# Gather indices through a small ScalarE copy, and one product moved ahead of the dot product's sum

## The chip, the cores and the metric

The kernel runs on one NeuronCore of a Trainium2 chip. The metric is the device time of one execution in microseconds (us). Before the change it is 5222.7 us, the median of three runs (5202.25 to 5230.44). The profile that is read here comes from one execution of its own: 5204.84 us in all, 5203.0 us from the first to the last instruction of the program.

## What is computed

One layer of an equivariant graph network: 12,500 nodes of 160 features (64 scalars, 32 vectors of three parts) and 400,000 edges, sorted by their target. Each edge takes the mapped row `y` of its source node, weighs it with weights that a small network makes from 16 edge features, multiplies it with four further edge features, and adds it to its target node.

```python
h = jnp.maximum(_layernorm(x, axis=-1), 0.0)
y0, y1 = x0 @ W_l1_0, einsum('nuc,uv->nvc', x1, W_l1_1)      # per node
w = silu(edge_length_embedded @ fc_W1) @ fc_W2                # per edge: w_a, w_b, w_c, w_d
ys0, ys1 = y0[edge_src], y1[edge_src]                         # the gather
mid_a = w_a * ys0 * e0
mid_d = w_d * einsum('euc,ec->eu', ys1, e1)                   # the dot product
mid_b = (w_b * ys0)[:, :, None] * e1[:, None, :]
mid_c = (w_c * e0)[:, :, None] * ys1
z = zeros.at[edge_dst].add(concatenate(mid_a, mid_d, mid_b, mid_c))
out = x + C_S * s + C_X * (z @ W_l2)
```

## The kernel before

**Stages.** A first stage (to about 218 us) normalises the nodes and writes `y` to the table `y_d` in HBM. The edge stage takes all the rest. A short last stage stores what is left.

**Tiles and batches.** 128 edges make a tile, four tiles a batch (`GT` = 4): 3125 tiles, 782 batches. In 22 of them (every 32nd) the rows are made again on the core instead of being gathered (`made`); the other 760 batches are gathered, by 3037 gathers of 128 rows of 640 bytes (the last batch is shorter).

**Edge stage.** One Python loop over `b` (L774) writes out the order of three engines by hand:

- **TensorE (PE)**: `weigh(b + 2)` makes the weights of a batch in the PSUM bank `pw` (L566, eight matmul passes; there are two such banks). `sums(b)` adds the finished products of a batch into `pz` through selection matrices (L603). `turn`, `map_sums` (every four batches or so) and `hidden` (every second batch, L550) use two further banks `px`.
- **ScalarE (ACT)**: `weigh` ends with a copy of three edge features next to the weights in `pw` (L567). This copy waits for the matmuls of its batch, and the queue is in order, so everything behind it waits too: what leaves PSUM (`all_leave`: `zs` L609, `za` L621, `os` L634 and L635, `hT` L555), then the four lifts of the batch (`lift_rows`, `yge`, L484).
- **VectorE (DVE)**: `dots_of(b + 1)` multiplies (L489) and sums (L491) the dot product; `products(b + 1)` makes `both` (L495), and then four pieces of `pr` (L496, L497, L500, L501). `weigh` may write a `pw` bank again when L501 of the batch that used it is done.
- **GpSimd (POOL)**: `load(b + 8)` issues the four gathers of a batch (L540). Its queue is not in the hand-written order, but it runs in program order. Each gather reads its row numbers from a column of `src_sb`.
- **SyncE (SP)** loads the edge features (`xe`, `raw`).

**What a gather waits for.** The gathered rows lie in nine buffers (`yg`, L135). Batch `c` takes the buffer that the ninth gathered batch before it had. Its first gather waits until VectorE has read that one for the last time (`both`, L495) and ScalarE has lifted it (L484). So within the loop the gathers that are issued in the code for batch `b + 10` follow, in time, `both` and the lift of batch `b + 1`. The other three gathers of a batch wait for nothing that is late.

Of the kernel before, what the change touches and what calls it, by code (L numbers as in the profile page):

```python
# [10 lines left out]
F32 = mybir.dt.float32  # L11
I32 = mybir.dt.int32
AF = mybir.ActivationFunctionType
# [5 lines left out]
P = 128  # L19
M0 = 64  # L20
M1 = 32
# [5 lines left out]
GT = 4  # L27
BT = 32
WN = 128
TG = 12  # L30
EG = 8
WIDE = 3, 5
GN = 8
HN = 2
# [9 lines left out]
def kernel(  # L44
# [19 lines left out]
    nc = tc.nc  # L64
# [11 lines left out]
    NB = (T + GT - 1) // GT  # L76
# [28 lines left out]
    def made(b):  # L105

        return b // RS - 1 if b % RS == 0 and 0 < b <= nr * RS else None
# [20 lines left out]
    src_sb = const.tile([P, TP], I32, name="src_sb")  # L128
# [3 lines left out]
    tile_i = const.tile([P, NG], I32, name="tile_i")  # L132
    far_i = const.tile([1, 1], I32, name="far_i")

    ygp = ctx.enter_context(tc.tile_pool(name="yg", bufs=9))  # L135

    ld = ctx.enter_context(tc.tile_pool(name="ld", bufs=2))
    NQ = -(-NU // EG)
# [126 lines left out]
    def load_xe(blk):  # L265

        if blk not in blocks:
            xe = ld.tile([P, 512], F32, name="xe")
            v = e16[blk * P:(blk + 1) * P, :].rearrange("(s k f) (h c) -> k s (f h) c", s=4, k=2, h=2)
            for k in range(2):  # L270
                nc.sync.dma_start(xe[:, 256 * k:256 * (k + 1)], v[k])
            blocks[blk] = xe
# [210 lines left out]
        for k in range(n):  # L483
            nc.scalar.activation(yge[:, k, :], yg[:, k, :], AF.Copy, scale=e4v[:, k, 0:1])  # L484

    def dot(tmp, wt, yg, n):

        y1 = yg[:, :n, M0:].rearrange("p t (c u) -> p t c u", c=3)
        nc.vector.tensor_tensor(tmp[:, :n, 0:3, :], y1, wt[:, :n, NW:NW + 3].unsqueeze(3).to_broadcast([P, n, 3, M1]),  # L489
                                ALU.mult)  # L490
        nc.vector.tensor_reduce(tmp[:, :n, 3, :], tmp[:, :n, 0:3, :].rearrange("p t c u -> p t u c"), AX.X, ALU.add)  # L491

    def multiply(pr, both, tmp, wt, yg, yge, n):

        nc.vector.tensor_mul(both[:, :n, :], wt[:, :n, 96:160], yg[:, :n, 0:M0])  # L495
# [5 lines left out]
        nc.vector.tensor_mul(pr[:, :n, 96:192].rearrange("p t (c u) -> p t c u", c=3),  # L501
                             wt[:, :n, M0:96].unsqueeze(2).to_broadcast([P, n, 3, M1]),
                             yge[:, :n, M0:].rearrange("p t (c u) -> p t c u", c=3))

    with (
# [3 lines left out]
        tc.tile_pool(name="hid", bufs=4) as hid,  # L509
        tc.tile_pool(name="post", bufs=2) as post,  # L510
        tc.tile_pool(name="made", bufs=2) as mk,
        tc.tile_pool(name="banks", bufs=1, space=PSUM) as banks,
    ):
        (hids, rows, lifted, dots, wts, sels, z_ps, z_sb, zT, o_sb, prs) = ({} for _ in range(11))
        leaving = []
        pws = [banks.tile([P, GT, 256], F32, name=f"pw{i}") for i in range(2)]
        pzs = [banks.tile([P, 512], F32, name=f"pz{i}") for i in range(2)]
        pxs = [banks.tile([P, 512], F32, name=f"px{i}") for i in range(2)]
# [4 lines left out]
            return pxs[turns["px"] % 2]  # L523

        K = TG // GT
        AHEAD = 8

        def tiles_of(b):
            return list(range(b * GT, min((b + 1) * GT, T)))

        def load(b):
            load_xe(b * GT // BT)
            r = made(b)
            if r is not None:
                rows[b] = xms[r]
                return
            yg = ygp.tile([P, GT, D], F32, name="yg")
            rows[b] = yg
            for k, t in enumerate(tiles_of(b)):
                nc.gpsimd.indirect_dma_start(  # L540
                    out=yg[:, k, :], out_offset=None, in_=y_d,
                    in_offset=bass.IndirectOffsetOnAxis(ap=src_sb[:, t:t + 1], axis=0))

        def hidden(s):

# [12 lines left out]
        def weigh(b):  # L558
            hT = hids[b // 2]
            pw = pws[b % 2]  # L560
            n = len(tiles_of(b))
            for k in (0, 2, 1, 3):
                if k < n:
                    r = slice(FC_H * (k // 2), FC_H * (k // 2 + 1))
                    o = P * (b % 2 * 2 + k % 2)
                    nc.tensor.matmul(pw[:, k, 0:NW], hT[r, o:o + P], w2[r, :], start=True, stop=True)  # L566
            nc.scalar.activation(pw[:, :n, NW:NW + 3], e4_of(b)[:, :n, 1:4], AF.Copy)  # L567
            wts[b] = pw
# [10 lines left out]
        def select(u, pz):  # L579

            n = min(TG, T - u * TG)
            sels[u] = selp.tile([P, TG, WN], F32, name="sel")
            nc.vector.tensor_tensor(sels[u][:, 0:n, :], pz[:, ZC:].unsqueeze(1).to_broadcast([P, n, WN]),  # L583
                                    drel[:, u * TG:u * TG + n].unsqueeze(2).to_broadcast([P, n, WN]), ALU.is_equal)

        def dots_of(b):
            dots[b] = part.tile([P, GT, 4, M1], F32, name="tmp")
            dot(dots[b], wts[b], rows[b], len(tiles_of(b)))

        def products(b):  # L590
            pr = prod.tile([P, GT, ZC], F32, name="pr")
            both = part.tile([P, GT, M0], F32, name="both")
            multiply(pr, both, dots.pop(b), wts.pop(b), rows.pop(b), lifted.pop(b), len(tiles_of(b)))
            prs[b] = pr

        def sums(b):
# [146 lines left out]
        def all_leave():  # L743
            todo = leaving[:]
            leaving.clear()
            for f in todo:
                f()

        order = tc.manual_schedule(engines={mybir.EngineType.PE, mybir.EngineType.Activation, mybir.EngineType.DVE})
        with order:  # L750
            e4_load(0)
            for b in range(min(AHEAD, NB)):
                load(b)
            relate_edges(0, part, lim)
            for s in range(3):
                hidden(s)
                all_leave()
            if NQ == 1:
                any_far(next_px()[0:1, 0:1])
            for b in range(min(2, NB)):  # L760
                weigh(b)
                lift_rows(b)
            for pz in pzs:
                nc.vector.tensor_copy(pz[:, ZC:], iota[:, 0:WN])
            dots_of(0)
            products(0)
            select(0, pzs[0])
            last_batch = [(t - 1) // GT for t in ends]
            turns_at, maps_at, adds_at = {}, {}, {}
            for g, e in enumerate(last_batch):  # L770
                turns_at.setdefault(e + 1, []).append(g)
                maps_at.setdefault(e + 2, []).append(g)
                adds_at.setdefault(e + (4 if e + 4 < NB else 3), []).append(g)
            for b in range(NB + 3):  # L774
                u, k = divmod(b, K)
                due(at_start, b)
                if b + AHEAD < NB:
                    load(b + AHEAD)
                if b < NB:
                    q, r = divmod(b, EG * K)  # L780
                    if r == 0:
                        e4_load(q + 1)
                    if r == EG * K - 8 and q + 1 < NQ:
                        relate_edges(q + 1, part, lim)
                    if r == EG * K - 4 and q + 2 == NQ:
                        any_far(next_px()[0:1, 0:1])
                if b + 2 < NB:
                    weigh(b + 2)
                all_leave()
                due(on_scalar, b)  # L790
# [24 lines left out]
    with (  # L815
# [11 lines left out]
        with tc.For_i(0, n, 1) as _:  # L827
# [4 lines left out]
            with tc.For_i(0, TP // GT, 1) as g:  # L832
# [31 lines left out]
                dot(tmp, pw, yg, GT)  # L864
                pr = fp.tile([P, GT, ZC], F32, name="f_pr")
                both = fp.tile([P, GT, M0], F32, name="f_both")
                multiply(pr, both, tmp, pw, yg, yge, GT)
# [81 lines left out]
```

## Time and profile before

| | |
|---|---|
| time, median of three runs | 5222.7 us (5202.25 to 5230.44) |
| the profiled execution: its time, its span | 5204.84 us, 5203.0 us |
| mean granted TensorE clock | 0.857 of full speed |
| gathers, packets moved by their queue | 3037 in the edge stage, 256.20 MB in all |
| DMA traffic | 64 GB/s over the span |

In a timeline row stand: start in us, duration in us, engine, line, operation, tiles (output <- inputs), shapes, how many instructions the row merges, and in brackets the idle time of that engine just before and what ended it. "issue" as the one that ended it means that the profile shows no event that did. In a group row the numbers behind the bar are the busy time, the mean of one instruction in ns, and the idle time before the group's instructions with what ended most of it. In the rows of one source line the three numbers with slashes are the shortest, median and longest duration in ns, and behind them the first and last start in us. In the list of waits a row gives the sum in us, how many waits, and the longest.

### The profile page before, as it was taken

The numbers are of one execution on the slowest core, as the hardware profiler recorded it, in microseconds if no ns is written. First come the engines' busy times: TensorE is split into PE (matmuls) and PEld (weight loads), VectorE is DVE, ScalarE is ACT, GpSimd is POOL, SyncE is SP. The second block draws the span as 40 slices with busy tenths as digits, with TensorE's granted clock in tenths as the row PEclk, the third lists the DMA queues.
The fourth block names the chain that finished last, engine by engine and source line by source line (L and its number), as shares of the span: only waits on it lengthen the run. The fifth ranks groups of instructions, "written<-read, shape, count | busy, mean of one in ns | idle before, by whom it ended". The sixth has DMA issues, their size and how long they took to land. (4 is left out here: it accounts for less than half of the span.)

```text
span 5203.0 us, 55078 instructions
## 1 busy us (share of the span) xinstructions
PE 4180.4 (80%) x16329; PEld 2384.2 (46%) x16329; DVE 3441.9 (66%) x7529; ACT 1764.7 (34%) x5580; POOL 2959.6 (57%) x3137
## 2 busy tenths in 40 slices
PE   4478888787888888888888878888888888888888
PEld 3334444444444444444444444444444444544444
DVE  4456667666666666776666666676767666766667
ACT  3323333333333333332333333333333333333333
POOL 4455655555555555555555555555555555655553
PEclk7778888888888888888888888888888888888888
DMA  5322222222222222222222222222222222232222
GB/s 180 115 57 58 61 58 62 58 60 60 57 60 59 60 61 57 59 61 60 57 60 58 60 57 57 60 60 58 60 54 61 58 59 57 61 94 57 57 57 58
DMA packets 227720, 333.84 MB, mean 64 GB/s; under 512 B 54714, under 2 KB 171526, under 8 KB 227158
## 3 DMA queue, kind: packets, MB, share of 16 engines
q0 software_dynamic: 150000, 256.20, 19.9%
q1 hardware_dynamic: 63618, 65.63, 4.0%
q10 hardware_dynamic: 13796, 8.44, 0.5%
q8 instruction: 130, 2.13, 0.2%
q14 instruction: 176, 1.44, 0.1%
HBM read 306.83 MB, written 23.22 MB: 63 GB/s over the span
## 5 line engine op out<-in xcount | busy, mean ns | idle before, releaser
L540 POOL DMA_INDIRECT yg<-y_d,src_sb x3037 | 2871.3, 945 | 2115.7 <-ACT yge L484 784.9
L603 PE MATMUL pz<-pr,sel 128*128 128x384 f32 x6250 | 2510.0, 548 | 58.4 <-issue 54.7
L603 PEld LDWEIGHTS pz<-pr,sel 128*128 128x128 f32 x6250 | 1259.2, 212 | 1032.0 <-issue 491.5
L489 DVE TENSOR_TENSOR tmp<-yg,pw 128x384 f32<-128x384 f32 x760 | 418.6, 551 | 1523.1 <-ACT pw L567 1292.7
L567 ACT ACTIVATE pw<-raw 128x12 f32<-128x12 f32 x782 | 141.9, 182 | 3289.3 <-issue 2801.2
L484 ACT ACTIVATE yge<-yg,raw 128x160 f32<-128x160 f32 x3037 | 1044.0, 421 | 0.0
L566 PE MATMUL pw<-w,hT 64*128 64x192 f32 x6250 | 839.5, 392 | 73.7 <-issue 24.1
L566 PEld LDWEIGHTS pw<-w,hT 64*128 64x128 f32 x6250 | 572.6, 212 | 545.1 <-issue 313.4
L497 DVE TENSOR_TENSOR pr<-both,pw 128x768 f32<-128x768 f32 x782 | 737.9, 944 | 0.0
L550 PE MATMUL px<-xe,w 32*128 32x512 f32 x782 | 522.9, 756 | 189.4 <-ACT os L635 137.1
L491 DVE TENSOR_REDUCE tmp<-tmp 128x128 f32<-128x384 f32 x782 | 464.1, 594 | 26.9
L583 DVE TENSOR_TENSOR sel<-pz,drel 128x1536 f32<-128x1536 f32 (+1 forms) x261 | 455.2, 1744 | 0.0
L501 DVE TENSOR_TENSOR pr<-pw,yge 128x384 f32<-128x384 f32 x782 | 428.0, 547 | 0.0
L617 PE MATMUL px<-ident,zs 128*128 128x128 f32 x555 | 112.7, 319 | 358.9 <-ACT zs L609 341.3
L500 DVE TENSOR_TENSOR pr<-pw,yge 128x256 f32<-128x256 f32 x782 | 326.6, 418 | 13.0 <-ACT yge L484 12.3
L495 DVE TENSOR_TENSOR both<-pw,yg 128x256 f32<-128x256 f32 x760 | 314.8, 414 | 0.0
L550 PEld LDWEIGHTS px<-xe,w 32*128 32x128 f32 x782 | 130.7, 209 | 345.5 <-ACT os L635 163.4
L630 PE MATMUL px<-wc,za 128*128 128x96 f32 x1110 | 165.5, 289 | 145.3 <-ACT za L621 137.7
L617 PEld LDWEIGHTS px<-ident,zs 128*128 128x128 f32 x555 | 74.2, 159 | 446.9 <-ACT zs L609 395.9
L630 PEld LDWEIGHTS px<-wc,za 128*128 128x128 f32 x1110 | 161.5, 205 | 207.4 <-ACT za L621 155.1
L555 ACT ACTIVATE hT<-px 128x512 f32<-128x512 f32 x391 | 229.3, 587 | 1.9 <-PE px L550 1.7
L496 DVE TENSOR_TENSOR pr<-pw,tmp 128x128 f32<-128x128 f32 x782 | 219.4, 281 | 0.0
(118 smaller groups left out, 1739.2 us busy)
## 6 DMA issues: line engine op xcount, KB each, us to landing
yg<-y_d,src_sb POOLq DMA_INDIRECT x3037
xe<-in_e SPq DMA_DIRECT2D x196, 128.0 KB
y_d<-ys ACTq DMA_DIRECT2D x12, 640.0 KB
xr_d<-xr SPq DMA_DIRECT2D x22, 320.5 KB
acc<-in_x SPq DMA_DIRECT2D x11, 640.0 KB
xm<-xr_d SPq DMA_DIRECT2D x22, 320.0 KB
out<-acc SPq DMA_DIRECT2D x11, 640.0 KB
raw<-in_e SPq DMA_DIRECT2D x32, 192.0 KB
```

Of the source, the lines that this page charges most:

```text
L484: nc.scalar.activation(yge[:, k, :], yg[:, k, :], AF.Copy, scale=e4v[:, k, 0:1])
L489: nc.vector.tensor_tensor(tmp[:, :n, 0:3, :], y1, wt[:, :n, NW:NW + 3].unsqueeze(3).to_broadcast([P, n, 3, M1]), ALU.mult)
L491: nc.vector.tensor_reduce(tmp[:, :n, 3, :], tmp[:, :n, 0:3, :].rearrange("p t c u -> p t u c"), AX.X, ALU.add)
L497: nc.vector.tensor_mul(pr[:, :n, 192:ZC].rearrange("p t (c u) -> p t c u", c=3), both[:, :n, :].unsqueeze(2).to_broadcast([P, n, 3, M0]), ...
L500: nc.vector.tensor_mul(pr[:, :n, 0:M0], wt[:, :n, 0:M0], yge[:, :n, 0:M0])
L501: nc.vector.tensor_mul(pr[:, :n, 96:192].rearrange("p t (c u) -> p t c u", c=3), wt[:, :n, M0:96].unsqueeze(2).to_broadcast([P, n, 3, M1]) ...
L540: nc.gpsimd.indirect_dma_start(out=yg[:, k, :], out_offset=None, in_=y_d, in_offset=bass.IndirectOffsetOnAxis(ap=src_sb[:, t:t + 1], axis=0))
L550: nc.tensor.matmul(ph, w1[r, :], xe[r, :], start=True, stop=True)
L566: nc.tensor.matmul(pw[:, k, 0:NW], hT[r, o:o + P], w2[r, :], start=True, stop=True)
L583: nc.vector.tensor_tensor(sels[u][:, 0:n, :], pz[:, ZC:].unsqueeze(1).to_broadcast([P, n, WN]), drel[:, u * TG:u * TG + n].unsqueeze(2).to ...
L603: nc.tensor.matmul(z_ps[g], sels[t // TG][:, t % TG, :], pr[:, k, :], start=first, stop=last)
L630: nc.tensor.matmul(px[:, lo:hi], za[:, k, :], wc[:, k, lo:hi], start=k == 0, stop=k == 1)
```

## The change

```diff
+YB = 9
-    ygp = ctx.enter_context(tc.tile_pool(name="yg", bufs=9))
+    ygp = ctx.enter_context(tc.tile_pool(name="yg", bufs=YB))
...
-    def dot(tmp, wt, yg, n):
+    def dot(tmp, both, wt, yg, n):
...
         nc.vector.tensor_tensor(tmp[:, :n, 0:3, :], y1, wt[:, :n, NW:NW + 3]..., ALU.mult)
+        nc.vector.tensor_mul(both[:, :n, :], wt[:, :n, 96:160], yg[:, :n, 0:M0])
         nc.vector.tensor_reduce(tmp[:, :n, 3, :], tmp[:, :n, 0:3, :]..., AX.X, ALU.add)
...
-    def multiply(pr, both, tmp, wt, yg, yge, n):
-        nc.vector.tensor_mul(both[:, :n, :], wt[:, :n, 96:160], yg[:, :n, 0:M0])
+    def multiply(pr, both, tmp, wt, yge, n):
...
+        tc.tile_pool(name="ids", bufs=YB + 3) as idp,
...
-        AHEAD = 8
+        AHEAD = YB + 1
...
+        def name_rows(b):
+            if made(b) is None:
+                ids[b] = idp.tile([P, GT], I32, name="ids")
+                n = len(tiles_of(b))
+                nc.scalar.activation(ids[b][:, :n], src_sb[:, b * GT:b * GT + n], AF.Copy)
...
         def load(b):
-            load_xe(b * GT // BT)
...
-                    in_offset=bass.IndirectOffsetOnAxis(ap=src_sb[:, t:t + 1], axis=0))
+                    in_offset=bass.IndirectOffsetOnAxis(ap=ids[b][:, k:k + 1] if b in ids else src_sb[:, t:t + 1],
+                                                        axis=0))
...
             e4_load(0)
-            for b in range(min(AHEAD, NB)):
+            for blk in range(min(AHEAD - 1, NB - 1) * GT // BT + 1):
+                load_xe(blk)
+            for b in range(min(YB, NB)):
                 load(b)
...
             dots_of(0)
+            if YB < NB:
+                load(YB)
             products(0)
...
                 if b + AHEAD < NB:
-                    load(b + AHEAD)
+                    load_xe((b + AHEAD) * GT // BT)
...
                 if b + 2 < NB:
                     weigh(b + 2)
+                if b + AHEAD < NB:
+                    name_rows(b + AHEAD)
                 all_leave()
...
                     products(b + 1)
                     if k == K - 1:
                         select(u + 1, pzs[(group_at[b * GT] + 1) % 2])
+                if b + AHEAD < NB:
+                    load(b + AHEAD)
```

Three things change. First, on ScalarE a copy of four row numbers for each of 128 partitions (`name_rows`) is put right behind the copy L567 of `weigh(b + 2)`, and the gathers of batch `b + 10` read their row numbers from it; those of the first ten batches still read `src_sb`. Second, on VectorE `both` is made between the dot product's multiplication and its sum. Third, the gathers of batch `b + 10` stand in the code behind `products(b + 1)` of the same pass, where they stood at the head of pass `b + 2`; nine batches of gathers instead of eight, and a tenth behind the first dot product, stand ahead of the loop; the loads of `xe` are issued two passes earlier. The number of `yg` buffers stays nine.

More of the change, by code (lines that the diff above doesn't have):

```diff
@@ L514 @@
         (hids, rows, lifted, dots, wts, sels, z_ps, z_sb, zT, o_sb, prs) = ({} for _ in range(11))
-        leaving = []
+        leaving, ids = [], {}
         pws = [banks.tile([P, GT, 256], F32, name=f"pw{i}") for i in range(2)]
@@ L586, in dots_of @@
         def dots_of(b):
-            dots[b] = part.tile([P, GT, 4, M1], F32, name="tmp")
-            dot(dots[b], wts[b], rows[b], len(tiles_of(b)))
+            tmp = part.tile([P, GT, 4, M1], F32, name="tmp")
+            both = part.tile([P, GT, M0], F32, name="both")
+            dot(tmp, both, wts[b], rows.pop(b), len(tiles_of(b)))
+            dots[b] = tmp, both
         def products(b):
             pr = prod.tile([P, GT, ZC], F32, name="pr")
-            both = part.tile([P, GT, M0], F32, name="both")
-            multiply(pr, both, dots.pop(b), wts.pop(b), rows.pop(b), lifted.pop(b), len(tiles_of(b)))
+            tmp, both = dots.pop(b)
+            multiply(pr, both, tmp, wts.pop(b), lifted.pop(b), len(tiles_of(b)))
             prs[b] = pr
@@ L863 @@
                 tmp = fp.tile([P, GT, 4, M1], F32, name="f_tmp")
-                dot(tmp, pw, yg, GT)
                 pr = fp.tile([P, GT, ZC], F32, name="f_pr")
                 both = fp.tile([P, GT, M0], F32, name="f_both")
-                multiply(pr, both, tmp, pw, yg, yge, GT)
+                dot(tmp, both, pw, yg, GT)
+                multiply(pr, both, tmp, pw, yge, GT)
                 for k in range(GT):
```

## The prediction

> **What bounds the kernel now.** I read the busy shares first, then the costliest groups, and then the timelines of single engines, because the shares name no bound.
>
> ```profile
> span 5203.0 us, 55078 instructions
> PE 4180.4 (80%) x16329; PEld 2384.2 (46%) x16329; DVE 3441.9 (66%) x7529; ACT 1764.7 (34%) x5580; POOL 2959.6 (57%) x3137
> L567 ACT ACTIVATE pw<-raw 128x12 f32<-128x12 f32 x782 | 141.9, 182 | 3289.3 <-issue 2801.2
> L540 POOL DMA_INDIRECT yg<-y_d,src_sb x3037: 940/946/1101, 217.9 to 5153.8; - x190
> ```
>
> No engine is full. ScalarE stands still for 3289.3 us ahead of the little copy L567, and for 2801.2 us of that the profile names no releaser, although the copy waits only for the matmuls of its own batch and for VectorE's use of the same bank. The gathers fill the time from 217.9 to 5153.8 us. Now one stretch, POOL's timeline:
>
> ```profile
> 1783.00 0.94 POOL L540 DMA_INDIRECT yg<-y_d,src_sb  x1 [4.75 <-ACT zs L609]
> 1784.25 0.94 POOL L540 DMA_INDIRECT yg<-y_d,src_sb  x1 [0.30 <-DVE pr L501]
> ...
> 1796.74 0.94 POOL L540 DMA_INDIRECT yg<-y_d,src_sb  x1 [0.30 <-issue]
> 1802.62 0.94 POOL L540 DMA_INDIRECT yg<-y_d,src_sb  x1 [4.94 <-ACT yge L484]
> ...
> 1816.42 0.95 POOL L540 DMA_INDIRECT yg<-y_d,src_sb  x1 [0.30 <-issue]
> 1822.14 0.94 POOL L540 DMA_INDIRECT yg<-y_d,src_sb  x1 [4.77 <-ACT zs L609]
> ```
>
> Twelve gathers, three batches, follow each other at (1796.74 - 1783.00) / 11 = 1.25 us; then comes a pause of 5.88 us from start to start; then twelve more. Next to it the matmuls of `weigh` and the copy that waits for them:
>
> ```profile
> 1792.78 0.92 PE L566 MATMUL pw<-w,hT 64*128 64x192 f32 x8
> 1800.71 2.07 PE L550 MATMUL px<-xe,w 32*128 32x512 f32 x2 [4.23 <-ACT os L635]
> 1802.71 1.65 PE L566 MATMUL pw<-w,hT 64*128 64x192 f32 x8
> 1808.60 0.92 PE L566 MATMUL pw<-w,hT 64*128 64x192 f32 x8
> 1813.28 0.92 PE L566 MATMUL pw<-w,hT 64*128 64x192 f32 x8
> ```
>
> ```profile
> 1800.14 0.18 ACT L567 ACTIVATE pw<-raw 128x12 f32<-128x12 f32 x1 [10.55 <-issue]
> 1804.45 0.18 ACT L567 ACTIVATE pw<-raw 128x12 f32<-128x12 f32 x1 [2.31 <-issue]
> 1809.62 0.18 ACT L567 ACTIVATE pw<-raw 128x12 f32<-128x12 f32 x1 [3.20 <-issue]
> 1819.66 0.18 ACT L567 ACTIVATE pw<-raw 128x12 f32<-128x12 f32 x1 [8.24 <-issue]
> ```
>
> The matmuls that end at 1804.36 and 1809.52 are answered 0.09 and 0.10 us later. Those that end at 1793.70 and 1814.20 are answered 6.44 and 5.46 us later. The answered ones fall 1.7 and 6.9 us into a run of gathers, the late ones 10.7 and 11.6 us into it; and both late copies come 3.40 and 3.24 us after the start of the run's last gather (1796.74, 1816.42). So I read it thus: **a long unbroken run of gathers holds TensorE's signal back until the run is over.** With it ScalarE stands still, then VectorE (no `pw`), then TensorE itself (the 4.23 us ahead of 1800.71). The run ends because POOL uses up what it is allowed, and is allowed more only when the late signal has gone on its way to the next release of a buffer:
>
> ```profile
> 1800.76 1.38 ACT L484 ACTIVATE yge<-yg,raw 128x160 f32<-128x160 f32 x4
> 1800.95 0.59 DVE L491 TENSOR_REDUCE tmp<-tmp 128x128 f32<-128x384 f32 x1
> 1801.46 0.41 DVE L495 TENSOR_TENSOR both<-pw,yg 128x256 f32<-128x256 f32 x1
> ```
>
> From L567 at 1800.14 it takes until 1801.87 to the end of `both` and until 1802.14 to that of the lifts; POOL starts at 1802.62, 2.48 us after the copy. The run's cycle is 13.75 + 3.40 + 2.48 = 19.63 us for three batches. All pauses together: 5153.8 - 217.9 = 4935.9 us, less 3036 x 1.25 = 3795 us of pace, leaves **1141 us**. That is what can be won. In the same stretch no engine is a bound yet:
>
> ```profile
> 217.90:5153.80 4935.90, 4042.37 (x15559) 2273.62 (x15556) 3304.82 (x7052) 1656.28 (x5307) 2870.39 (x3037) 0.86 0.24 60
> ```
>
> TensorE is busy for 4042 us of it, at a granted clock of 0.86.
>
> **The change, part by part.**
>
> *The new wait.* The gathers of batch b + 10 now wait for ScalarE's copy behind L567 of batch b + 2, beside `both` and the lift of batch b + 1, as before. While the signal of b + 2 is held, POOL may therefore finish batch b + 9 and no more, where before it could also do b + 10: one batch less of run. Behind the waiting gather stand only further gathers. And when the signal comes, `both` and the lifts of b + 1 have long been done, since VectorE and ScalarE were idle; so the next gather starts after the copy alone. Its delay from L567: 0.12 us to the next ScalarE instruction (L634 follows at 1800.26 in the rows of the part below), 0.18 us for a copy of L567's kind (128x12; no row shows 128x4 integers), and POOL's start, 1802.62 - 1802.14 = 0.48 us behind the lifts. I take 0.7 us, against 2.48 now; bounds 0.6 and 0.8 move the sum by 38 us each way.
>
> *How long runs become.* After a release at u, TensorE's next signal comes about 4.3 us later (1804.36 against 1800.14), 3.6 us into the new run, where the rows answer at once. That allows a second batch. The one after it (1809.52, 9.4 us after u) falls 8.7 us into the run, nearer to the late rows (10.7, 11.6) than to 6.9, so I take it as held, until the eighth gather is over. So **runs of eight** instead of twelve. What a run of eight has to wait at its end, from its last gather to L567, two rows show:
>
> ```profile
> 836.95 0.95 POOL L540 DMA_INDIRECT yg<-y_d,src_sb  x1 [0.30 <-issue]
> 839.27 0.18 ACT L567 ACTIVATE pw<-raw 128x12 f32<-128x12 f32 x1 [7.00 <-issue]
> 4841.28 0.95 POOL L540 DMA_INDIRECT yg<-y_d,src_sb  x1 [0.30 <-issue]
> 4844.15 0.18 ACT L567 ACTIVATE pw<-raw 128x12 f32<-128x12 f32 x1 [6.88 <-issue]
> ```
>
> 2.32 and 2.87 us; I take 2.6, with 2.32 as the lower end and the 3.40 of a run of twelve as the upper. A pause then adds 2.6 + 0.7 - 1.25 = 2.05 us to the pace, in 3037 / 8 = 380 runs: 779 us instead of 1141, a gain of **362 us**. Ends: 1.77 x 380 = 673 (gain 468) and 2.85 x 380 = 1083 (gain 58).
>
> *The copies.* Some 750 copies on ScalarE, 0.18 us each, 135 us beside 3289 us of idle time. What stands behind one, and who waits for that: `all_leave`, for which TensorE waits.
>
> ```profile
> 1800.26 0.21 ACT L634 ACTIVATE os<-px 128x64 f32<-128x64 f32 x1
> ...
> PE px L617 <- ACT zs L609: 341.3, 82, 9.7
> PE px L630 <- ACT za L621: 137.7, 27, 9.8
> PE px L550 <- ACT os L635: 137.1, 37, 6.1
> PE px L689 <- ACT os L635: 65.3, 17, 6.6
> ```
>
> 163 such waits, each longer by the 0.12 us that an instruction takes on that queue: **20 us**. If no other wait covered any of the 750, it would be 90 us.
>
> *`both` ahead of the sum.* VectorE does the same instructions. `both` ends some 0.5 us sooner (it takes the place of L491, 1800.95 to 1801.46), but it is no longer the last thing that the gather waits for. The sum now stands right ahead of L496, which needs it, where L491 stood right behind L489; that exchange is bounded by the idle time of L491 in the row below, 27 us either way, and lies under VectorE's waits for `pw`. I take nothing.
>
> ```profile
> L491 DVE TENSOR_REDUCE tmp<-tmp 128x128 f32<-128x384 f32 x782 | 464.1, 594 | 26.9
> L489 DVE TENSOR_TENSOR tmp<-yg,pw 128x384 f32<-128x384 f32 x760 | 418.6, 551 | 1523.1 <-ACT pw L567 1292.7
> DVE tmp L489 <- DMA yg<-y_d,src_sb: 49.1, 20, 6.3
> ```
>
> *Later gathers, earlier `xe`.* A gather is issued up to a batch later, with some eight batches (50 us) left before its rows are lifted. Waits for landing rows are 49.1 us now; I leave them so (if the lead were too short they would grow with it). The Trainium skill, "DMA: Bandwidth & Descriptors", section "Rules for kernel authors", speaks against this part: issue a DMA early and wait for it late. By it the sum would be worse by some share of those 49 us, at most doubled; the row bears the rule out only where the lead is used up, which 20 waits show. The 196 `xe` loads go out two passes earlier on SP, past nothing that anybody waits for (no wait for `xe` stands in the list), and cost nothing; had that cover gone, the TensorE rows would show L550 waiting for them. The start, with ten batches that still read `src_sb`, issues the same gathers in the same order.
>
> *Sum.* 5203 - 362 + 20 = 4861 us of span; 1.84 us lie outside it, and the median of the runs is 17.9 us above the profiled execution's 5204.84. So I expect **4880 us**. Own range, from the two ends: 4775 to 5185.
>
> **The rivals.**
>
> *Longer runs stay.* If the third signal gets through (the row at 6.9 us did), runs keep twelve gathers: 253 x (3.40 + 0.7 - 1.25) = 721 us, a gain of 420: 5203 - 420 + 20 + 20 = 4823 us. For it: the first signals come soon after a release. Against: from 10.7 us on all rows shown are late. It is still a win; only the quicker start counts. If signals were never held again, POOL's pace alone would leave 4102 us; the runs of four below speak against it.
>
> *Lock step, slower.* Each signal may be held to the end of the single batch that it allowed. The rows show that a run of four can hold one:
>
> ```profile
> 2633.77 1.65 PE L566 MATMUL pw<-w,hT 64*128 64x192 f32 x8
> ...
> 2637.43 0.94 POOL L540 DMA_INDIRECT yg<-y_d,src_sb  x1 [0.30 <-issue]
> 2639.78 0.18 ACT L567 ACTIVATE pw<-raw 128x12 f32<-128x12 f32 x1 [6.58 <-issue]
> ```
>
> Matmuls ending at 2635.42 are answered 4.36 us late, 2.35 us after the fourth gather. If every batch goes so, 760 pauses of 2.35 + 0.7 - 1.25 = 1.80 us make 1368 us: a loss of 227, so 5203 + 227 + 20 + 20 = 5470 us. The point from which it decides: with some six in ten batches alone in their runs (1368 x 0.6 + 779 x 0.4 = 1132) the gain of the eights is eaten up. Against it: there the run before had ended only 2.96 us earlier; after a full release the rows at 1804.45 and 1809.62 are punctual.
>
> *Nothing changes.* If the matmuls themselves end late, and the run of gathers merely stops because nothing releases a buffer, then the new wait takes away nothing, and the time stays at 5223 us (5243 with the copies). The Trainium skill, "Perfetto Trace Analysis", section "Per-instruction lifecycle: what the profiler-reported window actually captures", bears on this: a matmul's end is an estimate, and the signal goes out only when PSUM has confirmed the writes. By that rule the 6.44 us would be TensorE's own tail, and the sum zero. Against it: the same eight matmuls are answered in 0.1 us twice, and lateness goes with the age of the run.
>
> **How the numbers follow.** My forecast 0.53, longer runs 0.18, lock step 0.17, nothing changes 0.12. A measurement of this kernel tells about 0.5% (26 us) from no change. Forecast and longer runs are faster: 0.71; nothing changes gives 0.12 for the same; lock step 0.17 for slower. The range reaches from below the longer runs (some signals never held) to just above no change, 4700 to 5240, and leaves out lock step.
>
> **What would show it.** Right: the idle time ahead of L567 without a releaser falls well below 2801 us; POOL's long pauses shrink from 5.9 to some 3.3 us and come every eight gathers; the next gather starts about 0.7 us after L567; TensorE's granted clock rises a little, as its pauses shorten. Wrong: pauses after every fourth gather (lock step); late answers that outlast the run by more than 4 us, or late answers with POOL idle (then the gathers aren't what holds the signal); a gather that starts 2 us behind L567 (then another wait comes last).

## The result, and the profile after

| | before | changed |
|---|---|---|
| time, median | 5218.41 us (4 runs, 5202.25 to 5230.44) | 4862.31 us (4 runs, 4849.66 to 4875.87) |
| ratio | | 0.9322, 95% interval 0.9291 to 0.9353: faster |
| profiled execution: time, span | 5204.84, 5203.0 us | 4849.66, 4847.9 us |
| granted TensorE clock | 0.857 | 0.89 |

The forecast was 4880 us, with a range of 4700 to 5240. To read the numbers further down: in the later sets of runs (e5 to f3) the kernel **before** took 3964 to 3973 us, in all its runs alike, and there TensorE's signals were punctual (ScalarE's copy follows the end of its matmuls by about 0.1 us); in the runs of this table, in e1 to e4 and in g1 it took 5214 to 5222 us and the signals were late. Every kernel is compared below with the kernel before of its own set.

The page of the changed kernel, its span and busy shares:

```profile
span 4847.9 us, 55829 instructions
...
PE 4065.3 (84%) x16329; PEld 2330.0 (48%) x16329; DVE 3445.3 (71%) x7529; ACT 1836.9 (38%) x6330; POOL 2970.6 (61%) x3137
```

The busy microseconds of VectorE and GpSimd are those of before within 11 us, TensorE's are 115 fewer, ScalarE's are 72 more, with the 750 copies. What went is idle time. The groups of instructions (behind the last bar stand the idle time ahead of a group and what ended it):

```profile
L547 POOL DMA_INDIRECT yg<-y_d,ids x2997 | 2844.7, 949 | 1685.0 <-ACT ids L537 791.0 <-issue 767.5 <-DVE drel L194 24.6
...
L537 ACT ACTIVATE ids<-src_sb 128x4 int32<-128x4 int32 x750 | 142.1, 189 | 0.8
...
L575 ACT ACTIVATE pw<-raw 128x12 f32<-128x12 f32 x782 | 141.7, 181 | 2859.3 <-issue 2131.1 <-remote 615.0 <-ACT yge L485 62.8
...
L490 DVE TENSOR_TENSOR tmp<-yg,pw 128x384 f32<-128x384 f32 x760 | 417.8, 550 | 1146.5 <-ACT pw L575 1050.2 <-issue 89.8 <-DMA yg<-y_d,ids 4.0
...
L493 DVE TENSOR_REDUCE tmp<-tmp 128x128 f32<-128x384 f32 x782 | 455.2, 582 | 0.0
...
L497 DVE TENSOR_TENSOR pr<-pw,tmp 128x128 f32<-128x128 f32 x782 | 227.8, 291 | 27.1
```

L575 is the copy that was L567, L547 the gather that was L540. The copy's wait without a named releaser fell from 2801.2 to 2131.1 us, but the part of its wait put down to `remote` rose from 300.2 to 615.0, so the sum is the safer number: 2859.3 us, where it was 3289.3. VectorE's wait for the weights fell from 1292.7 to 1050.2. The late signals are still there. The gathers now wait for the `ids` copy (791.0 us), where the chain led through `both` and the lifts. The 26.9 us ahead of the sum have become 27.1 us ahead of L497. Now one pause, in the timelines of GpSimd, ScalarE and TensorE:

```profile
1802.90 0.94 POOL L547 DMA_INDIRECT yg<-y_d,ids  x1 [2.03 <-ACT ids L537]
...
1811.71 0.94 POOL L547 DMA_INDIRECT yg<-y_d,ids  x1 [0.30 <-issue]
1814.92 0.95 POOL L547 DMA_INDIRECT yg<-y_d,ids  x1 [2.26 <-ACT ids L537]
```

```profile
1807.00 0.18 ACT L575 ACTIVATE pw<-raw 128x12 f32<-128x12 f32 x1 [2.58 <-issue]
...
1814.35 0.18 ACT L575 ACTIVATE pw<-raw 128x12 f32<-128x12 f32 x1 [5.28 <-issue]
1814.47 0.19 ACT L537 ACTIVATE ids<-src_sb 128x4 int32<-128x4 int32 x1
```

```profile
1805.99 0.92 PE L574 MATMUL pw<-w,hT 64*128 64x192 f32 x8
...
1809.61 0.92 PE L574 MATMUL pw<-w,hT 64*128 64x192 f32 x8
```

The matmuls that end at 1806.91, four gathers into the run, are answered at 1807.00. Those that end at 1810.53 are answered 3.82 us later, 2.64 us after the start of the run's eighth and last gather (1811.71). The copy of row numbers follows 0.12 us behind, and the next gather starts 0.57 us after L575, where it was 2.48 us. The pause is 3.21 us from start to start instead of 5.88.

Counted in the two traces from 400 us on, over the starts of all gathers and over the copies L567 and L575. A pause is more than 1.4 us from start to start, a run is what lies between two pauses. A copy is called late when ScalarE had nothing to do and stood idle for more than 0.3 us past the end of the copy's own matmuls:

| | before | changed |
|---|---|---|
| pauses, mean length | 368, 4.25 us | 378, 3.23 us |
| over the pace of 1.25 us, together | 1103 us | 749 us |
| pauses in which a late copy falls, mean length | 237, 5.31 us | 299, 3.48 us |
| over the pace, together | 962 us | 666 us |
| all other pauses, mean length | 131, 2.32 us | 79, 2.30 us |
| over the pace, together | 141 us | 83 us |
| runs of 4, 8, 12 and 16 gathers | 154, 34, 123, 20 | 118, 127, 108, 2 |
| mean length of a run | 7.9 gathers | 7.7 gathers |
| late copies, together | 309, 1571 us | 338, 1344 us |

1103 - 749 = 354 us: nearly the whole difference of the two spans (355.1 us). There are about as many pauses as before, but that is a sum of two kinds. Those with a late copy are 1.83 us shorter, close to the 1.91 us by which the way from the copy to the next gather became shorter (2.48 to 0.57), and there are 62 more of them; the others are as long as before, and there are 52 fewer.

### The profile page after: what moved, and what is told of

It reads as the page before. It is cut to its first block, busy times and chain, and to the rows that moved or that the text cites. A ratio compares the mean times of both kernels' runs of the same rounds, so it can differ in the third digit from the quotient of the medians.

```text
span 4847.9 us, 55829 instructions
## 1 busy us (share of the span) xinstructions
PE 4065.3 (84%) x16329; PEld 2330.0 (48%) x16329; DVE 3445.3 (71%) x7529; ACT 1836.9 (38%) x6330; POOL 2970.6 (61%) x3137
## 5 line engine op out<-in xcount | busy, mean ns | idle before, releaser
L547 POOL DMA_INDIRECT yg<-y_d,ids x2997 | 2844.7, 949 | 1685.0 <-ACT ids L537 791.0
L613 PE MATMUL pz<-pr,sel 128*128 128x384 f32 x6250 | 2443.8, 536 | 62.2 <-issue 41.6
L613 PEld LDWEIGHTS pz<-pr,sel 128*128 128x128 f32 x6250 | 1226.3, 207 | 1000.0 <-issue 428.8
L490 DVE TENSOR_TENSOR tmp<-yg,pw 128x384 f32<-128x384 f32 x760 | 417.8, 550 | 1146.5 <-ACT pw L575 1050.2
L575 ACT ACTIVATE pw<-raw 128x12 f32<-128x12 f32 x782 | 141.7, 181 | 2859.3 <-issue 2131.1
L574 PE MATMUL pw<-w,hT 64*128 64x192 f32 x6250 | 804.4, 379 | 70.0 <-DVE pr L502 37.3
L574 PEld LDWEIGHTS pw<-w,hT 64*128 64x128 f32 x6250 | 548.9, 204 | 511.8 <-issue 273.1
L558 PE MATMUL px<-xe,w 32*128 32x512 f32 x782 | 486.5, 707 | 55.1 <-ACT os L645 40.2
L640 PE MATMUL px<-wc,za 128*128 128x96 f32 x1110 | 181.2, 306 | 225.7 <-ACT za L631 216.2
L492 DVE TENSOR_TENSOR both<-pw,yg 128x256 f32<-128x256 f32 x760 | 316.2, 416 | 0.0
L497 DVE TENSOR_TENSOR pr<-pw,tmp 128x128 f32<-128x128 f32 x782 | 227.8, 291 | 27.1
```

The costliest lines, as they stand in the source:

```text
L547: nc.gpsimd.indirect_dma_start(out=yg[:, k, :], out_offset=None, in_=y_d, in_offset=bass.IndirectOffsetOnAxis(ap=ids[b][:, k:k + 1] if b i ...
L558: nc.tensor.matmul(ph, w1[r, :], xe[r, :], start=True, stop=True)
L613: nc.tensor.matmul(z_ps[g], sels[t // TG][:, t % TG, :], pr[:, k, :], start=first, stop=last)
L640: nc.tensor.matmul(px[:, lo:hi], za[:, k, :], wc[:, k, lo:hi], start=k == 0, stop=k == 1)
```

## The experiments

**e1, the gathers read `src_sb` again.** Everything else of the change stays, the place of the gathers and of `both` too.

```diff
-  in_offset=bass.IndirectOffsetOnAxis(ap=ids[b][:, k:k + 1] if b in ids else src_sb[:, t:t + 1],
+  in_offset=bass.IndirectOffsetOnAxis(ap=src_sb[:, t:t + 1],
...
-                if b + AHEAD < NB:
-                    name_rows(b + AHEAD)
```

> The changed kernel without the ids copy: the gathers read src_sb again, at the same later place in the program, so they wait for `both` and the lift of the batch whose yg buffer they take. Theory (the gain is the shorter way from TensorE's late signal to the next gather, 0.65 us instead of 2.54, at some 380 pauses): the delay comes back and with it the whole gain, 5220 us, within 30. Rival (the order of the work or the place of the gathers made the gain): 4862 us, within 25.

Measured: 5175.53 us beside 5213.82, ratio 0.9931 (0.9915 to 0.9948). Without the copy nearly all of the gain is gone, so neither the new place nor `both` made most of it. The time falls 15 us short of the theory's band (5190 to 5250). The timelines of ScalarE and GpSimd:

```profile
1810.82 0.18 ACT L575 ACTIVATE pw<-raw 128x12 f32<-128x12 f32 x1 [7.76 <-issue]
...
1811.42 1.38 ACT L485 ACTIVATE yge<-yg,raw 128x160 f32<-128x160 f32 x4
```

```profile
1813.06 0.94 POOL L547 DMA_INDIRECT yg<-y_d,src_sb  x1 [4.55 <-ACT pw L575]
```

From the copy to the next gather it is 2.24 us here and not 2.48. It is the lifts that are waited for: they end at 1812.80, 0.26 us ahead of the gather, while `both` (L492), made ahead of the sum, ended at 1811.93. Before the change `both` ended last more often: of its 368 pauses, 208 end 0.74 us after a `both` and 137 end 0.27 us after a lift; of the 378 pauses of e1 it is 34 and 334. So `both` ahead of the sum does shorten the way here, until the lifts stop it. The 38 us that e1 is faster than the kernel before are what it and the new place give together; they weren't run apart.

**e2, `both` behind the sum again**, the copy of row numbers stays.

```diff
-        nc.vector.tensor_mul(both[:, :n, :], wt[:, :n, 96:160], yg[:, :n, 0:M0])
         nc.vector.tensor_reduce(tmp[:, :n, 3, :], ...)
+        nc.vector.tensor_mul(both[:, :n, :], wt[:, :n, 96:160], yg[:, :n, 0:M0])
```

> The changed kernel with `both` behind the dot product's sum again; the ids copy stays. Theory (`both` ahead of the sum costs and brings nothing, since the 27 us of waiting go with the place and not with the instruction, and the gathers no longer wait for `both` last): 4862 us, within 25. Rival (it is `both` that lets the gathers go sooner): each of some 380 pauses is longer by the sum's 0.58 us, 220 us, so 5080 us.

Measured: 4861.11 us, ratio 0.9321 (0.9303 to 0.9339). The second part of the change does nothing beside the first. The 27 us stand ahead of the sum again:

```profile
L492 DVE TENSOR_REDUCE tmp<-tmp 128x128 f32<-128x384 f32 x782 | 464.7, 594 | 26.9
```

**e3, the copy of row numbers later on ScalarE**, behind what leaves PSUM and behind the lifts.

```diff
-                if b + AHEAD < NB:
-                    name_rows(b + AHEAD)
                 all_leave()
                 due(on_scalar, b)
                 if b + 2 < NB:
...
                     lift_rows(b + 2)
+                if b + AHEAD < NB:
+                    name_rows(b + AHEAD)
```

> The changed kernel with the ids copy issued behind the leaving tiles and the lift of the batch on ScalarE: permission for the gathers comes some 1.8 to 2 us later after the same signal of TensorE. Theory (only this delay matters): 380 pauses x 1.9 us = 720 us at most and about 360 us where the lift has to wait anyway, so 5200 us, from 5100 to 5500. Rival (what matters is which signal of TensorE the gathers wait for, and so how many may be issued behind one): 4862 us, within 40.

Measured: 5188.93 us, ratio 0.9950 (0.9928 to 0.9973). The gathers wait for the same signal of TensorE as in the changed kernel, and as many batches of gathers may follow it, and still nearly all of the gain is gone. The runs are those of before again: 52 of eight gathers, 131 of twelve, 24 of sixteen. In the timelines of ScalarE and GpSimd the next gather starts 2.33 us after the late copy:

```profile
1808.40 0.18 ACT L575 ACTIVATE pw<-raw 128x12 f32<-128x12 f32 x1 [8.09 <-issue]
...
1810.27 0.20 ACT L537 ACTIVATE ids<-src_sb 128x4 int32<-128x4 int32 x1
```

```profile
1810.73 0.94 POOL L547 DMA_INDIRECT yg<-y_d,ids  x1 [4.65 <-ACT pw L575]
```

Put in order of that delay: 0.57 us gives 4862 us, 2.24 gives 5176, 2.33 gives 5189, 2.48 gives 5214. Between the outer two lie 352 / 1.91 = 184 us of time per microsecond of delay; by that line the inner two would be 5169 and 5186. The rows shown are typical: over all pauses in which a late copy falls the median delay is 0.57, 2.27, 2.37 and 2.48 us. In e1 to e4 the time follows this delay and nothing else that was varied.

**e4, one batch less ahead.**

```diff
-        AHEAD = YB + 1
+        AHEAD = YB
...
-            if YB < NB:
-                load(YB)
```

> The changed kernel with AHEAD 9 instead of 10: the gathers and the ids copies of a batch come one loop pass later, one batch less may be issued behind one signal of TensorE. Theory (only the time from the signal to the next gather matters, not the number of batches allowed): 4862 us, within 40. Rival (the prediction's step: the length of a run of gathers is set by the batches allowed, and one less makes runs of eight into runs of four, whose pause of 2.3 us then comes 760 times): from 5100 us to 5470 us.

Measured: 4844.72 us, ratio 0.9287 (0.9272 to 0.9303). Allowing one batch less does not shorten the runs: 352 pauses are left, 741 us over the pace, 298 of them with a late copy. So the length of a run isn't set by how many batches are allowed behind a signal.

**e5, e6 and e7, a memset of a spare tile behind each gather**: 128x64 in the changed kernel, 128x320 in it, 128x64 in the kernel before.

```diff
+    pace = const.tile([P, 64], F32, name="pace")
...
                 nc.gpsimd.indirect_dma_start(...)
+                nc.gpsimd.memset(pace, 0.0)
```

> The changed kernel with a GpSimd memset of 128x64 of a spare tile behind each gather: GpSimd gets 3037 instructions more, of 0.14 us each (estimate between the 0.10 us of 128x1 and the 0.20 us of 128x128), so a gather comes every 1.40 us instead of 1.25. Theory (it is the density of the gathers that holds TensorE's signal back: in the traces a late signal comes as if each gather took 1.41 us to be dealt with, and a signal behind five gathers or fewer in the last 8.75 us is punctual): nearly all signals become punctual, the 750 us of pauses go, and GpSimd's pace sets the time: 3037 x 1.41 + 380 us of start and end = 4660 us, from 4580 to 4760, less than now although GpSimd has more to do. Rival (the signal is late for another reason; the memsets only lengthen GpSimd's work): 4862 + 3037 x 0.14 = 5290 us.

> The same with a memset of 128x320 (estimate 0.36 us), a gather every 1.62 us. Theory: all signals are punctual, the pauses are gone, and only GpSimd's pace counts: 3037 x 1.62 + 380 = 5300 us, from 5050 to 5400; the wait of ScalarE's copy behind `weigh` that no engine is blamed for falls from 2131 us to less than 500 us beyond what GpSimd's pace makes. Rival (pauses as now): 4862 + 3037 x 0.37 = 5990 us.

> The kernel before, with the memset of 128x64 behind each gather and nothing else. Theory (density holds the signal): the signals are punctual here too, so the 2.54 us from the signal to the next gather are hidden behind a run that has not ended, and the time is close to the paced changed kernel's, 4680 us, up to 4850. Rival (the pauses stay): 5214 + 3037 x 0.14 = 5640 us.

Measured beside a kernel before of 3973.19 us: e5 4645.57 (ratio 1.1693, 1.1674 to 1.1713), e6 5274.52 (1.3275, 1.3248 to 1.3301), e7 4648.40 (1.1702, 1.1682 to 1.1721). All three lie near the theory's figures, and it is no evidence for it: the memsets did not pace the gathers. GpSimd's queue isn't part of the order written by hand, and nothing ties a memset of a spare tile to a gather, so they were issued far ahead. So this queue does not run in the order of the lines in the code, though the description of the kernel says that it runs in program order. In e5, the memset's line, and windows of 200 us with GpSimd's busy time and instructions, the granted clock, DMA share and GB/s:

```profile
L552 POOL MEMSET pace<- x3037: 143/152/266, 10.1 to 1585.2; 128x64 f32 x190
```

```profile
200.00:400.00 200.00, 146.73 (x456) 0.78 0.18 45
1400.00:1600.00 200.00, 145.63 (x456) 0.79 0.18 44
1600.00:1800.00 200.00, 151.52 (x160) 0.98 0.31 78
2500.00:2700.00 200.00, 151.47 (x160) 0.98 0.31 78
```

Until 1585 us the memsets crowd the gathers out; from then on 160 gathers run in 200 us, one each 1.25 us, without a pause, for some 3000 us. e7 does the same with the kernel before's own waits. An endless dense run thus holds no signal back here: no copy of e5 that found ScalarE idle starts more than 0.39 us after its matmuls. The theory that density alone does it has fallen.

**e8, no gathers of node rows at all**: three memsets in place of each, so the gathered rows of `y` are left out.

```diff
-                nc.gpsimd.indirect_dma_start(out=yg[:, k, :], ...)
+                nc.gpsimd.memset(yg[:, k, :], 0.0)
+                nc.gpsimd.memset(pace, 0.0)
+                nc.gpsimd.memset(pace, 0.0)
```

> The changed kernel with each gather of node rows replaced by three GpSimd memsets (the batch's own rows set to zero, a spare 128x448 twice), 1.24 us of work by the rows of the profile (0.22 + 2 x 0.46 and some 0.1 between); so the gathered rows of y are left out. Theory A (the gather's DMA, its descriptors and packets, holds TensorE's signal): signals punctual, nothing left of the late releases. Theory B (any dense work of GpSimd does it): the releases of ScalarE's copy behind `weigh` come 2 to 3 us after GpSimd's runs as now. The time itself decides nothing here.

Measured: 4259.37 us in one run. No copy that found ScalarE idle starts more than 0.38 us after its matmuls, but in this set none came later than 0.39 us with gathers either; it tells nothing apart.

**f1, the changed kernel as it is**, in a set where signals are punctual.

> The changed kernel as it is, once more, beside the kernel before: the runs with memsets stood beside a kernel before of 3973 us, where TensorE's signal came 0.02 us after `weigh` in 99 of 100 batches. Theory (the change gains only by making a late signal cheaper): where the kernel before takes about 3973 us the signals are punctual, there is nothing to shorten, and the changed kernel takes the same, 3975 us, from 3955 to 4010 (the 763 ids copies of 0.12 us on ScalarE, which has room). Rival (the shorter permission helps by itself): 0.93 x 3973 = 3700 us, which GpSimd's pace of 3037 x 1.25 = 3796 us forbids, so at best 3900 us. Where the kernel before takes about 5214 us, both expect 4862 us as measured.

Measured: 3962.96 us beside 3964.53, ratio **0.9997 (0.9987 to 1.0006)**. Page and groups of this run:

```profile
span 3961.3 us, 55829 instructions
...
PE 3689.1 (93%) x16329; PEld 2157.4 (54%) x16329; DVE 3446.2 (87%) x7529; ACT 1996.6 (50%) x6330; POOL 2975.6 (75%) x3137
```

```profile
L547 POOL DMA_INDIRECT yg<-y_d,ids x2997 | 2839.6, 947 | 912.8 <-issue 777.9 <-ACT yge L485 41.1 <-DVE both L492 17.4
...
L575 ACT ACTIVATE pw<-raw 128x12 f32<-128x12 f32 x782 | 137.6, 176 | 683.3 <-PE pw L574 451.5 <-issue 174.0 <-DVE tmp L493 17.7
```

The gathers wait for next to nothing but their own issue, 0.30 us each; 26 of them, 7.9 us in all, are put down to an `ids` copy, and the 750 copies cost nothing that can be seen. Of the 782 copies L575, 424 found ScalarE idle, and none of these starts more than 0.39 us after its matmuls. In the timelines of TensorE, ScalarE and GpSimd, 1.7 ms after the first gather:

```profile
1856.49 0.92 PE L574 MATMUL pw<-w,hT 64*128 64x192 f32 x8
```

```profile
1857.51 0.18 ACT L575 ACTIVATE pw<-raw 128x12 f32<-128x12 f32 x1 [2.40 <-PE pw L574]
```

```profile
1859.13 0.95 POOL L547 DMA_INDIRECT yg<-y_d,ids  x1 [0.30 <-issue]
```

Matmuls that end at 1857.41 are answered at 1857.51. The time is GpSimd's pace: the first gather at 139.7 us, 3036 x 1.252 = 3801 us, and 20 us behind the last.

**f2 and f3, a memset that can't run ahead**: it writes the rows that the gather then overwrites.

```diff
+                nc.gpsimd.memset(yg[:, k, 0:64], 0.0)
                 nc.gpsimd.indirect_dma_start(out=yg[:, k, :], ...)
```

> The changed kernel with a GpSimd memset of 128x64 on the rows that the gather then overwrites, ahead of each gather; it can't be issued ahead of its batch, as the memsets of a spare tile were. A batch takes GpSimd 4 x 1.25 + 4 x 0.2 = 5.8 us, 1.45 us for a gather. Where the kernel before takes about 5214 us (late signals): theory (density holds the signals): punctual signals, 782 batches... 760 gathered batches x 5.8 + 270 = 4680 us, from 4580 to 4780; rival (lateness has nothing to do with the gathers' density): 4862 + 760 x 0.8 = 5470 us. Where it takes about 3973 us (punctual signals): both expect GpSimd's pace alone, 3037 x 1.45 + 180 = 4580 us.

> The changed kernel with the memset on the rows ahead of each gather again, which beside a kernel before of 3964.53 us took 4211.28 us, that is 3037 x 0.08 us more; so a gather of this kernel comes every 1.33 us on the average. Where the kernel before takes about 5214 us this time: theory (the density of the gathers holds TensorE's signal, which is dealt with at some 1.41 us for a gather): fewer signals are late, the pauses shrink more than GpSimd's work grows, from 4500 to 4800 us; rival (lateness has nothing to do with the density): 4862 + 250 = 5110 us. Where it takes about 3964 us: 4211 us again, within 20.

Measured, with punctual signals both times: 4211.28 us beside 3964.53 (ratio 1.0622, 1.0605 to 1.0640) and 4209.74 beside 3964.48 (1.0618, 1.0587 to 1.0649). A gather comes every 1.33 us, less than the 1.45 expected. Here pacing is pure loss, as both views said.

**g1, that memset twice.**

> As the last run, with the memset twice: 0.17 us more of GpSimd's work for a gather, so one every 1.33 + 0.17 = 1.50 us on the average, above the 1.41 us that a gather seems to take where signals are late. Where the kernel before takes about 5214 us: theory (density holds the signal): punctual signals, 3037 x 1.50 + 180 = 4740 us, from 4650 to 4830; rival (density has no part): 4862 + 250 + 516 = 5630 us. Where it takes about 3964 us: GpSimd's pace alone, 4210 + 3037 x 0.17 = 4726 us, within 60.

Measured, this time with late signals: 4984.36 us beside 5221.77, ratio 0.9553 (0.9499 to 0.9608). Between the two expectations, so the rows have to tell. Groups, and GpSimd's timeline around the end of a batch:

```profile
L549 POOL DMA_INDIRECT yg<-y_d,ids x2997 | 2847.5, 950 | 1158.2 <-issue 868.6 <-ACT yge L485 127.5 <-DVE both L492 76.7
...
L485 ACT ACTIVATE yge<-yg,raw 128x160 f32<-128x160 f32 x3037 | 1245.0, 426 | 2177.6 <-DMA yg<-y_d,ids 2056.5 <-POOL yg L547 72.5 <-issue 29.9
...
L577 ACT ACTIVATE pw<-raw 128x12 f32<-128x12 f32 x782 | 133.4, 171 | 599.9 <-issue 228.5 <-PE pw L576 140.9 <-remote 133.7
```

```profile
1804.40 0.94 POOL L549 DMA_INDIRECT yg<-y_d,ids  x1 [0.31 <-issue]
...
1806.09 0.15 POOL L548 MEMSET yg<- 128x64 f32 x1
1806.79 0.95 POOL L549 DMA_INDIRECT yg<-y_d,ids  x1 [0.55 <-ACT yge L485]
```

The copy's wait without a releaser is 228.5 us, against 2131.1 in the changed kernel; 65 copies are late instead of 338, together 196 us instead of 1344. Part of that is no cure: only 225 copies found ScalarE idle here from 400 us on, against 648, because ScalarE is late itself, and a signal that it isn't waiting for can't be seen to be late. What g1 changes are the runs: with a breath at the end of a batch (2.39 us from start to start in the rows, where the pace would have 1.25) a run has 3.3 gathers on the mean instead of 7.7, though on the average the gathers come hardly further apart (1.56 us in g1, 1.51 in the changed kernel).

How much that matters can be counted in the traces. The copies that found ScalarE idle, from 400 us on, sorted by the time from the start of the run of gathers to the end of the copy's own matmuls:

| the matmuls end | before | changed | g1 | f1 |
|---|---|---|---|---|
| up to 4 us into a run | 63 of 300 late | 27 of 164 | 23 of 147 | 0 of 4 |
| 4 to 8 us into it | 92 of 185 | 117 of 247 | 12 of 41 | 0 of 8 |
| later in it | 150 of 151 | 166 of 166 | 9 of 9 | 5 of 383, by 0.39 us at most |
| in a pause | 4 of 35 | 28 of 71 | 21 of 28 | - |

Where signals are late at all, nearly every one that is due more than 8 us into a run is late, in g1 as well, and g1 has few of them. And the late ones mostly wait for the end of the run: of the 309 of before, 72 are answered while a gather of the same run is still to come. So under this condition lateness does go with the run of gathers, not with their average density. What joins the two is not shown: a trial without gathers under late signals is missing.

The gain of g1 is eaten up by the memsets themselves: a gather comes every 1.56 us on the average, 0.06 more than expected (0.55 us pass between the last memset and the gather), and now ScalarE waits for rows (2056.5 us) and not for weights. A lighter pace under late signals was not tried, and no version run here beats the changed kernel in either condition beyond the intervals: those of e4, 18 us faster, overlap with its own.

## Why the prediction was right, and where not

- **What bounds the kernel** ("a long unbroken run of gathers holds TensorE's signal back until the run is over"): borne out in the traces with late signals, where 150 of 151 signals of before that were due more than 8 us into a run were late (table of g1). It was read from four copies; in the whole trace a fifth of the signals due in the first 4 us are late too (63 of 300), and 72 of 309 late ones are answered before the run is over. And it was told as a property of the gathers, while f1 and e7 show the same density for 3000 us with no copy over 0.4 us late. A second condition is needed, which the kernels here did not set.
- **The new wait**, 0.7 us from the late copy to the next gather: 0.57 measured, in the pause shown and as the median of all. e1 and e3 undo it in two ways and lose 90 and 93% of the gain (0.0069 and 0.0050 of the 0.0678 stay). This is the step that carries the result. Its largest term was misread: 0.48 us for GpSimd's start "behind the lifts". The next gather starts 0.26 us after the end of the `ids` copy (1814.66 to 1814.92), and in the row of before it had been `both`, ended at 1801.87, that was waited for.
- **"One batch less of run", "runs of eight instead of twelve"**: this step failed. The reason given for shorter runs was that one batch less may follow a held signal. In e3 as many may follow it as in the changed kernel, and the runs are those of before; in e4 one batch less may follow it, and the pauses don't multiply. Runs of eight did become more common (34 before, 127 after), but with the shorter delay and not with the allowance, and 108 runs of twelve are left of 123. The stretch that I read had two runs of twelve next to each other, and I took them for the rule; 154 runs of before had four gathers. Why more, and shorter, pauses come with a shorter delay was not tested.
- **The sum** came within 30 us of the pauses measured, 779 against 749, and that is luck in part: 380 pauses of 2.05 us over the pace were forecast, all of one kind; there are 299 of 2.23 with a late copy and 79 of 1.05 without, and the 1141 us of before were measured and not built from runs.
- **The end of a run of eight**, 2.6 us from its last gather to the copy: 2.64 in the pause shown, and 2.64 as the median after the 127 runs of eight of the changed kernel. After runs of twelve the median is 3.30 in both kernels, after the 20 runs of sixteen of before 3.96. Each further gather thus adds some 0.16 us to the wait, which is an estimate from these medians; with the pace of 1.25 it gives the 1.41 us for a gather of which the expectations speak.
- **The copies, 20 us**: not seen. TensorE's waits that they were to lengthen became shorter, and under punctual signals the two kernels differ by 1.6 us in all. In the list of waits of the changed kernel the four that added up to 681.4 us (341.3 + 137.7 + 137.1 + 65.3) add up to 488.9:

```profile
PE px L640 <- ACT za L631: 216.2, 72, 5.5
PE px L627 <- ACT zs L619: 192.9, 68, 6.5
...
PE px L558 <- ACT os L645: 40.2, 23, 3.8
PE px L699 <- ACT os L645: 39.6, 13, 4.8
```

- **`both` ahead of the sum, nothing**: right (e2), and the bound of 27 us moved to the place that was named. Where no `ids` copy is waited for (e1), it takes `both` out of the way, and the lifts come last.
- **Later gathers**: cost nothing, as assumed; VectorE's wait for landing rows fell from 49.1 us to about 4, and e4 issues them later still without loss. The rule of the Trainium skill that spoke against it, "DMA: Bandwidth & Descriptors", section "Rules for kernel authors" (issue early, wait late), cost nothing to break while eight batches of lead were left.
- **Rivals.** Lock step would have shown as 760 pauses; there are 378. Longer runs would have kept 253 pauses of twelve, and that number was never there. The time forecast by "nothing changes" is ruled out under late signals, by 4862 against 5218 us. It came true under punctual ones (f1), for another reason than the one given: the matmuls do not end late, there is no wait to shorten. The Trainium skill, "Perfetto Trace Analysis", section "Per-instruction lifecycle: what the profiler-reported window actually captures", has the end of a matmul as an estimate; with punctual signals the copy follows that end by 0.10 us, so a tail that belongs to every such matmul is no explanation of 3 to 6 us.

## What to carry to other kernels

When an engine waits for a signal that the profile can't account for, two things can be done: make the signal punctual, or shorten the way from the signal to the work that it lets go. The second is cheap and certain where it is late (184 us per microsecond of delay here), and worth exactly nothing where it isn't. Time the kernel before again beside every new version, as a change that makes a condition of the machine cheaper shows its gain only while the condition holds; and look at the issue order of an experiment before reading its time, since a filler that nothing orders may run somewhere else.

## What the runs showed of the hardware

- **One program, two times.** The kernel before took 5199 to 5230 us in some sets and 3963 to 3974 in others, with no run in between. The single instructions take as long in both (in the changed kernel a gather 949 and 947 ns, by the rows of L547); the difference is TensorE's signals and the pauses behind them. It isn't a property of a chip alone: f3 (punctual) and g1 (late) ran on a chip of the same number. What sets the condition is open.
- **It begins with the program.** Under late signals the first gather of the edge stage of the changed kernel starts at 219.8 us, under punctual ones at 139.7. In the waits up to 130 us of the changed kernel, ScalarE stands still ahead of the copy of a tile that TensorE writes, four times and once for 29.1 us; in f1 it stands still there for 0.4 us in all:

```profile
ACT hT L406 <- remote: 55.8, 4, 29.1
```

- **The clock follows the waits.** The granted clock was 0.854 to 0.906 in the runs with late signals and 0.98 in f1, and it was 0.78 and then 0.98 within the one run of e5, where TensorE first lacked work (the memsets crowded the gathers out) and then had it. There the clock follows TensorE's pauses and does not make them.
- **Open:** whether the matmuls or only their signal come late. In the profile of before, TensorE is recorded as going on with eight matmuls of the next sums, up to 1796.48 us, while the next increment of TensorE's semaphore on record after the weights that ended at 1793.70 came at 1800.07. That speaks for the signal, but no run here could show it. ScalarE's signals to GpSimd are not held: in the changed kernel the gather starts 0.27 us after the end of the `ids` copy in nine of ten pauses. And the recording itself may take part: with late signals a share of the increments has no record (3746 of ScalarE's 5235 have one in the trace of before, 5962 of 5985 in f1), and an execution without recording was not tried.
